# Twelve ScalarE scalings for one VectorE product: four edits to the side work of a state-space scan

## Chip, core and metric

The kernel runs on one core of a Trainium2 chip. The metric is the device time of one execution in microseconds; the kernel before has a median of 9078.85 us over 13 runs (9040.54 to 9110.47). The engines are TensorE (PE, matrix products), VectorE (DVE), ScalarE (ACT), GpSimd (POOL) and SyncE (SP, which only issues transfers). Each engine works through its own instructions in the order in which they were emitted.

## What is computed

Four images of 96 channels and 64 x 64 pixels go through four layers, each added to its input:

- **Layer 0**, a selective state-space layer. Per image a norm, a projection to 192 channels and a 3x3 convolution give u. From u come, for four directions k, the step sizes delta and the vectors B and C. Then for each channel and each of 16 states `h = exp(delta*A)*h + (delta*u)*B` runs along the 4096 pixels, and `y = sum(h*C)`. The four directions are added, normalised, gated by z and projected.
- **Layer 1**, a deformable 3x3 convolution. A convolution gives for each pixel and each of nine taps an offset and a mask. Each tap is sampled at its shifted place: four neighbouring pixels, weighted by the bilinear weights times the mask, are added. A product with the weights follows.
- **Layers 2 and 3**: a Fourier mixing (a transform over 4096 tokens, a diagonal product, the transform back), a feed-forward net with inputs rounded to 8-bit floats, a linear attention over all tokens, and a second such feed-forward net.

## The kernel before

**The scan** (`Layer0.scan`) is the backbone: 4 images x 4 directions x 4 pieces of 1024 pixels x 24 groups of 8 channels = 1536 units. In one unit, with 8 channels x 16 states on the 128 partitions, ScalarE takes `exp` of the steps (`decay`, line 933, two units ahead of the scan), TensorE spreads delta*u over the states into PSUM (`inflow`, 939, one unit ahead, two buffers), VectorE multiplies that by B (`enter`, 953) and runs the recurrence (`recur`, 961), GpSimd saves the last column (`weigh`, 968) and multiplies by C (970), and TensorE folds the states (`total`, 989). ScalarE's queue also issues the 512 KB load `da` of each unit (912).

**Side work** is put between the units by two streams (`layers23`, lines 1702 to 1750). `ends` does layer 0 up to the scan for images 0 to 3 (`Layer0.before`) and then layers 2 and 3 image by image. `middle` does, for each image, the end of layer 0 (`behind`) and layer 1 (`Layer1.image`). `ends` begins with image b's layers 2 and 3 only once layer 1 of that image is done. When the scan is over, both streams go on with each other and the unit loop stands still (`alone`); `net.own_banks` is set from there on.

**The order** of all instructions is fixed when the program is made. Each step of a stream is a Python generator step that emits instructions and yields their assumed cost per engine. A `Clock` keeps the assumed end of each engine's work. `unit` moves the due time of the next unit on by `PACE`, the least unit time. `has_room` lets a step be emitted only while the engines it uses are at most `AHEAD` (3, 3, 5, 7 us for PE, DVE, ACT, POOL) beyond now, and at most `BESIDE` = 6 us of VectorE's side work go beside one unit. `go` (1725) offers the room to the two streams in reversed order, `middle` first.

**What the change touches:**

- `steps` (752) makes delta and delta*u for 512 pixels: TensorE product `pd`, five ScalarE activations (772 to 777), two GpSimd subtractions (780, 781), the VectorE sum `rl` = delta (783), the GpSimd product with u (786, 792; for the transposed direction with a strided view), then three ScalarE casts and TensorE products that split delta*u into three 16-bit parts. Each image has 48 such chains. `lw` has one buffer.
- `sample` (1284) handles three taps of 128 pixels at a time, 96 such groups an image: three indirect gathers by GpSimd (1301) fill `g` with 12 pixels of 96 channels on each partition, one VectorE product (1310) weights them, and TensorE transposes and adds the four corners (1327). After the scan VectorE adds the corners (1314, 1315) and TensorE only transposes. ScalarE evicts (1335), TensorE multiplies by the weights (1343).
- `chunk` in `Ffn.run` (1562) does 512 tokens: GpSimd rounds the input to 8 bits (1567), TensorE, ScalarE's eviction (1573), the bias (1578 by VectorE after the scan, 1582 by ScalarE within it), GpSimd rounds again (1585), TensorE, eviction (1591), bias (1594 or 1596), sum (1598).

Of the kernel before, what the change touches and what calls it, by code (L numbers as in the profile page):

```python
# [14 lines left out]
AF = mybir.ActivationFunctionType  # L15
# [4 lines left out]
B, C, H, W = 4, 96, 64, 64  # L20
# [152 lines left out]
class Step:  # L173
# [5 lines left out]
    def __init__(self, work, wait=0.0, holds=0, new=False, takes="", frees=""):  # L179
        self.work, self.wait, self.holds, self.new = work, wait, holds, new  # L180
        self.takes, self.frees = takes.split(), frees.split()


def cost(pe=0.0, dve=0.0, act=0.0, pool=0.0, **more):
    return Step((pe, dve, act, pool), **more)


def wait(us=0.0, **more):

    return Step((0.0,) * 4, us, **more)  # L190
# [10 lines left out]

MARGIN = 0.5

PACE = 4.7


class Clock:
# [19 lines left out]
    def unit(self, scanned):  # L227

        self.due += PACE
        self.idle, self.beside = max(scanned, self.due), 0.0  # L230
# [115 lines left out]
class Net:  # L346
# [3 lines left out]
    def __init__(self, ctx, tc, ins):  # L350
        self.tc, self.nc, self.ins = tc, tc.nc, ins
        nc = self.nc
        self.const = ctx.enter_context(tc.tile_pool(name="const", bufs=1))
        self.dram = ctx.enter_context(tc.tile_pool(name="scratch", bufs=1, space=DRAM))
        self.psum = ctx.enter_context(tc.tile_pool(name="mm", bufs=3, space=PSUM))
        for name in ("vecs", "ident", "cen96", "grp3", "add4"):
            setattr(self, name, self.load(name, self.const))

        self.to_row = {}
        for n in (C, DI):  # L360
            t = self.to_row[n] = self.const.tile([128, 65], F32, name=f"to_row{n}")
            nc.vector.memset(t, 0.0)
            nc.vector.memset(t[:, 1:2], 1.0 / n)
        self.eps = self.const.tile([128, 1], F32, name="eps")
        nc.vector.memset(self.eps, 1e-5)
        self.one = self.const.tile([128, 1], F32, name="one")
        nc.vector.memset(self.one, 1.0)
        self.minus_one = self.const.tile([128, 1], F32, name="minus_one")
        nc.vector.memset(self.minus_one, -1.0)
        self.exp_and_log()  # L370

        self.sampled = set()
        self.clock, self.known, self.streams, self.stream = Clock(), {}, [], None

        self.own_banks = None
# [164 lines left out]
class Layer0:  # L540
# [211 lines left out]
    def steps(self, b, ks, j, us, dtw, sm, xdbl):  # L752

        net = self.net
        nc = net.nc
        cs = slice(j * CH, (j + 1) * CH)
        tk = f"{b}_{j}_" + "".join(str(k) for k in ks)
        both = len(ks) == 2

        def tile_of(name, bufs):  # L760
            return sm.tile([128, CH], F32, name=f"{name}{tk}", tag=name, bufs=bufs)

        yield wait(new=True, takes="ex lw")


        pd = net.mm(f"pd{tk}")
        for k in ks:
            q = k % 2
            o, m = (pd[64 * q : 64 * q + 64], slice(128, DI)) if both else (pd, slice(0, 128))
            nc.tensor.matmul(o, lhsT=dtw[:, k, m], rhs=xdbl[q, j], start=True, stop=True)  # L770
        ex = tile_of("ex", 3)
        nc.scalar.activation(ex, pd, AF.Abs)
        nc.scalar.activation(ex, ex, AF.Exp, scale=-1.0)
        lw, w1 = tile_of("lw", 1), tile_of("w1", 1)
        nc.scalar.activation(lw, ex, AF.Ln, bias=net.one)
        nc.scalar.activation(w1, ex, AF.Identity, bias=net.one)
        nc.scalar.activation(w1, w1, AF.Identity, bias=net.minus_one)  # L777
        yield cost(pe=2.2 if both else 1.1, act=3.4, holds=1, takes="rl")
        rl = tile_of("rl", 2)
        nc.gpsimd.tensor_sub(w1, w1, ex)  # L780
        nc.gpsimd.tensor_sub(lw, lw, w1)  # L781
        yield cost(pool=2.8, holds=1)
        nc.vector.scalar_tensor_tensor(rl, pd, 0.0, lw, ALU.max, ALU.add)  # L783
        yield cost(dve=0.7, frees="lw")
        if not both and ks[0] % 2:
            nc.gpsimd.tensor_mul(
                ex.rearrange("p (w h) -> p w h", h=H),
                rl.rearrange("p (w h) -> p w h", h=H),
                us[1][:, j * NR : (j + 1) * NR, :],
            )  # L790
        else:
            nc.gpsimd.tensor_mul(ex, rl, us[2 if both else 0][:, cs])  # L792
        parts = ((0, 64, ks[0], 128), (64, 128, ks[1], 128)) if both else ((0, 128, ks[0], 0),)
        for p0, p1, k, c0 in parts:
            nc.sync.dma_start(self.de_d[b][k][c0 : c0 + p1 - p0, cs], rl[p0:p1])
        yield cost(pool=1.4, takes="du", frees="rl")

        du = sm.tile([128, 3, CH], BF16, name=f"du{tk}", tag="du", bufs=2)
        nc.scalar.copy(du[:, 0, :], ex)
        yield cost(act=0.6, new=True)  # L800
        pr = net.mm(f"pr{tk}")
        nc.tensor.matmul(pr, lhsT=net.ident, rhs=ex, start=True, stop=False)  # L802
        nc.tensor.matmul(pr, lhsT=self.minus, rhs=du[:, 0, :], start=False, stop=True)
        nc.scalar.copy(du[:, 1, :], pr)
        yield cost(pe=1.5, act=0.6, holds=1, frees="ex")
        nc.tensor.matmul(
            pr, lhsT=self.minus, rhs=du[:, 1, :], start=False, stop=True, skip_group_check=True
        )
        nc.scalar.copy(du[:, 2, :], pr)
        yield cost(pe=0.4, act=0.6)  # L810
        for p0, p1, k, c0 in parts:
            dst = self.du_d[b][k][:, c0 : c0 + p1 - p0, cs]
            nc.sync.dma_start(dst.rearrange("s c t -> c s t"), du[p0:p1])
        self.ready.update((b, k, both, j) for k in ks)
        yield wait(frees="du")
# [300 lines left out]
class Layer1:  # L1116
# [23 lines left out]
    def image(self, b):  # L1140
        tc = self.net.tc
        with tc.tile_pool(name=f"l1i{b}", bufs=1, side="right") as ix:
            idx = ix.tile([128, 288], U32, name=f"idx{b}", tag="idx")
            wt = ix.tile([128, 288, 4], F32, name=f"wt{b}", tag="wt")
            yield from self.before(b, idx, wt)
            yield from self.sample(b, idx, wt)
        self.net.sampled.add(b)

# [135 lines left out]
    def sample(self, b, idx, wt):  # L1284
        net = self.net
        tc, nc = net.tc, net.nc
        with tc.tile_pool(name=f"l1g{b}", bufs=1, side="right") as gp:
# [4 lines left out]
            def taps(t, k0):  # L1292
# [4 lines left out]
                cs = slice(j * 256, (j + 1) * 256)  # L1297
                g = gp.tile([128, 3, 4 * C], F32, name=f"g{key}", tag="g", bufs=6)
                for k in range(3):
                    n = 9 * t + k0 + k  # L1300
# [4 lines left out]
                        in_offset=bass.IndirectOffsetOnAxis(ap=idx[:, n : n + 1], axis=0),  # L1305
                    )
                    yield cost(pool=1.5, wait=7.0 * (k == 2))
                g4 = g.rearrange("p k (c d) -> p (k c) d", d=C)
                w4 = wt[:, 9 * t + k0 : 9 * t + k0 + 3, :].rearrange("p k c -> p (k c)")
                nc.vector.tensor_mul(g4, g4, w4.unsqueeze(2).to_broadcast([128, 12, C]))  # L1310
                added = net.own_banks is not None
                if added:

                    nc.vector.tensor_add(g[:, :, : 2 * C], g[:, :, : 2 * C], g[:, :, 2 * C :])
                    nc.vector.tensor_add(g[:, :, :C], g[:, :, :C], g[:, :, C : 2 * C])
                first = q == 0 and k0 == 0
                yield cost(dve=2.7 if added else 1.8, new=True, takes="st" if first else "")
                if first:
                    sts[j] = gp.tile([C, 9, 256], F32, name=f"st{b}_{j}", tag="st")
                st = sts[j]  # L1320
# [210 lines left out]
class Ffn:  # L1531
# [23 lines left out]
    def run(self, b, t):  # L1555
        net, n = self.net, self.n
        tc, nc = net.tc, net.nc
        with tc.tile_pool(name=f"fb{n}_{b}", bufs=1) as big, tc.tile_pool(name=f"fs{n}_{b}", bufs=2) as pool:
            tl = big.tile([C, L], F32, name=f"fl{n}_{b}", tag="tl")
            yield from normed(net, t, tl, f"f{n}_{b}", pool)  # L1560

            def chunk(j):
                yield wait(takes="xq")
                cs = slice(j * CH, (j + 1) * CH)
                key = f"f{n}_{b}_{j}"
                xq = pool.tile([C, CH], F8, name=f"xq{key}", tag="xq")
                nc.gpsimd.tensor_copy(xq, tl[:, cs], saturate=False)  # L1567
                yield cost(pool=0.8, new=True, takes="h16")
                h16 = pool.tile([128, 3, CH], F16, name=f"h16{key}", tag="h16")
                for g in range(3):  # L1570
                    ph = net.mm(f"ph{key}_{g}")
# [10 lines left out]
                        nc.scalar.activation(h16[:, g], h16[:, g], AF.Relu, bias=self.bias[:, g : g + 1])  # L1582
                    yield cost(act=2.1, takes="h8")
                h8 = pool.tile([128, 3, CH], F8, name=f"h8{key}", tag="h8")
                nc.gpsimd.tensor_copy(h8, h16, saturate=False)
                yield cost(pool=1.5, new=True, takes="o16", frees="h16")
                po = net.mm(f"po{key}")
                for g in range(3):
                    nc.tensor.matmul(po, lhsT=self.w2[:, g, :], rhs=h8[:, g], start=(g == 0), stop=(g == 2))
                o16 = pool.tile([C, CH], F16, name=f"o16{key}", tag="o16")  # L1590
# [106 lines left out]
def layers23(net, x2, out):  # L1697
# [4 lines left out]
    with ExitStack() as ctx:  # L1702
# [19 lines left out]
        streams = net.streams = [Stream(net, ends()), Stream(net, middle())]  # L1722
        clock = net.clock

        def go():

            return any([stream.step() for stream in reversed(streams)])

        def alone():

# [5 lines left out]
        for goes in l0.scan():  # L1736
# [3 lines left out]
            if clock.own is not None:  # L1740
                clock.due = max(clock.due, clock.own + PACE)
                clock.idle = max(clock.idle, clock.due)
# [32 lines left out]
```

## Time and profile before

| what | us |
|---|---|
| median of 13 runs | 9078.85 |
| the profiled execution | 9090.48 |
| its span, first to last instruction | 9088.7 |
| first and last scan (line 961) | 365 to 7907 |
| sampling of image 0, of 1, of 2 | 2559 to 3738, 4469 to 5502, 6374 to 7340 |
| sampling of image 3, after the scan | 8077 to 8534 |
| layers 2 and 3 of image 0, of 1 (within the scan) | 4752 to 6134, 6143 to 7555 |
| layers 2 and 3 of image 2 | 7563 to 8632 |
| layers 2 and 3 of image 3 (alone) | 8632 to 9089 |
| busy, of the span: PE, DVE, ACT, POOL | 73%, 77%, 46%, 70% |

A row for a group of instructions gives line, engine, operation, the tiles written and read, and shapes; then how many, their busy time and mean duration, the idle time of the engine just before them, and what ended it. A row for a stretch of time gives start and end, length, the busy time and count for each engine, the granted TensorE clock, the busy share of the transfer engines and GB/s. Busy shares are averages over stages with different limits, so they have to be read by stage.

### The profile page before, as it was taken

How to read it: one execution, taken by the hardware profiler on the slowest of the kernel's cores; microseconds unless marked ns; L12 is line 12 of the kernel's file. 1: busy time of each engine (PE TensorE's matmuls, PEld its weight loads, DVE VectorE, ACT ScalarE, POOL GpSimd, SP SyncE). 2: the span in 40 equal slices, each digit the busy share in tenths (PEclk: the TensorE clock that was granted, in tenths of full speed). 3: DMA queues.
4: the chain of work that ended last, by engine and by line, in shares of the span. 5: the costliest groups of instructions: out<-in, count | busy, mean ns of one | idle time of the engine just before them, and what ended most of it. 6: DMA issues, size and time to landing. Idle time of an engine off the chain costs nothing.

```text
span 9088.7 us, 93197 instructions
## 1 busy us (share of the span) xinstructions
PE 6601.8 (73%) x31960; PEld 2989.1 (33%) x31960; DVE 6955.7 (77%) x4932; ACT 4186.7 (46%) x5798; POOL 6389.0 (70%) x4755
## 2 busy tenths in 40 slices
PE   6664976697766668777667787777777777874687
PEld 2111311132222234211224554223554332462373
DVE  0367878887788889788789898988999998646514
ACT  4564667565554435556543324554333434321223
POOL 0486679766788989788799896765888966538501
PEclk8775977798777779877778888888888777886797
DMA  1466788777778788787788878677888776644210
GB/s 51 130 183 166 186 197 223 197 190 187 196 205 209 206 207 219 195 207 206 200 209 207 220 205 195 171 170 193 219 212 213 189 174 171 157 131 138 72 58 12
DMA packets 775967, 1608.21 MB, mean 177 GB/s; under 512 B 247809, under 2 KB 339357, under 8 KB 773382
## 3 DMA queue, kind: packets, MB, share of 16 engines
q10 hardware_dynamic: 244224, 843.17, 37.3%
q1 hardware_dynamic: 457542, 532.51, 22.0%
q0 software_dynamic: 73728, 226.57, 9.5%
q8 instruction: 255, 4.18, 0.2%
q14 instruction: 218, 1.79, 0.1%
HBM read 1345.62 MB, written 256.29 MB: 176 GB/s over the span
## 4 chain that ended last, share of the span: by engine, by line
PE 32%; DVE 19%; DMA 16%; POOL 15%; issue 10%; ACT 6%; SPq 2%; ACTq 1%; DVEq 0%; POOLq 0%
DVE hh L961 8%; POOL hh L970 7%; DVE db L953 5%; PE pc L692 4%; PE py L989 4%; POOL g L1301 3%; PE ps L1327 3%; PE f L1421 3%; PE db L939 3%; DMA du<-du 3%; DMA da<-de 2%; PE pd L1343 2%; DVE g L1310 2%; DMA m<-in_dft 2%; DMA bc<-bcd 1%
## 5 line engine op out<-in xcount | busy, mean ns | idle before, releaser
L970 POOL TENSOR_TENSOR hh<-hh,bc 128x1024 f32<-128x1024 f32 x1536 | 3657.5, 2385 | 340.7 <-DVE hh L961 222.6
L961 DVE TENSOR_TENSOR_SCAN hh<-da,st,db 128x1024 f32<-128x1024 f32 x1152 | 2700.2, 2344 | 190.0 <-PE py L989 59.3
L953 DVE TENSOR_TENSOR db<-db,bc 128x1024 f32<-128x1024 f32 x1536 | 1864.2, 1214 | 534.0 <-PE db L939 532.0
L933 ACT ACTIVATE da<-da,w_al 128x1024 f32<-128x1024 f32 x1536 | 1740.4, 1147 | 841.8 <-DMA da<-de 403.2
L939 PE MATMUL db<-du,rep 96*128 96x512 bf16 x3072 | 1094.1, 445 | 785.8 <-DVE hh L961 711.0
L1301 POOL DMA_INDIRECT g<-table,idx x1152 | 1342.8, 1166 | 363.5 <-issue 226.1
L989 PE MATMUL py<-hh,w_fold 128*32 128x512 f32 x6144 | 1101.8, 748 | 91.2 <-POOL hh L970 59.1
L1327 PE MATMUL ps<-w_ident,g 128*96 128x128 f32 x3744 | 639.7, 333 | 509.0 <-issue 299.1
L961 DVE TENSOR_TENSOR_SCAN hh<-da,db 128x1024 f32<-128x1024 f32 x384 | 876.8, 2283 | 54.8 <-PE py L989 19.2
L939 PEld LDWEIGHTS <-rep 96*128 96x128 bf16 x3072 | 279.7, 107 | 1756.2 <-issue 1106.8
L1310 DVE TENSOR_TENSOR g<-g,wt 128x1152 f32<-128x1152 f32 x384 | 705.0, 1838 | 102.2 <-DMA g<-table,idx 101.9
L1335 ACT COPY st<-ps 96x384 f32<-96x384 f32 x384 | 182.8, 476 | 1298.2 <-PE ps L1327 1155.0
L1327 PEld LDWEIGHTS ps<-w_ident,g 128*96 128x96 f32 x3744 | 519.3, 155 | 786.6 <-issue 420.2
L968 POOL COPY st<-hh 128x1 f32<-128x1 f32 x1152 | 303.5, 263 | 518.0 <-DVE hh L961 477.7
L780 POOL TENSOR_TENSOR w<-w,ex 128x512 f32<-128x512 f32 x192 | 245.6, 1279 | 500.2 <-ACT w L777 499.6
L692 PE MATMUL pc<-pad,wc 96*128 96x512 f32 x1152 | 544.7, 612 | 48.3 <-DMA wc<-wc_d 44.1
L783 DVE SCALAR_TENSOR_TENSOR rl<-pd,lw 128x512 f32<-128x512 f32 x192 | 131.2, 683 | 422.2 <-POOL lw L781 404.4
L802 PE MATMUL pr<-ex,w_ident 128*128 128x512 f32 x384 | 284.7, 832 | 153.7 <-POOL ex L792 64.5
L1567 POOL CAST xqf<-fl 96x512 fp8e5<-96x512 f32 x64 | 44.4, 702 | 496.7 <-DVE fl L1525 459.2
L989 PEld LDWEIGHTS py<-hh,w_fold 128*32 128x32 f32 x6144 | 160.9, 121 | 616.4 <-issue 370.7
L770 PE MATMUL pd<-xd,w_dtw 103*64 103x512 f32 (+1 forms) x512 | 277.9, 830 | 69.8 <-DMA w_dtw<-in_dtw 32.1
L692 PEld LDWEIGHTS pc<-pad,wc 96*128 96x128 f32 x1152 | 217.5, 195 | 321.9 <-issue 299.4
(249 smaller groups left out, 9205.0 us busy)
## 6 DMA issues: line engine op xcount, KB each, us to landing
da<-de ACTq DMA_DIRECT2D x1536, 512.0 KB
du<-du SPq DMA_DIRECT2D x512, 192.0 KB
bc<-bcd SPq DMA_DIRECT2D x128, 512.0 KB
du<-du SPq DMA_DIRECT2D x128, 384.0 KB
y<-yb SPq DMA_DIRECT2D x384, 128.0 KB
de<-rl SPq DMA_DIRECT2D x128, 256.0 KB
m<-in_dft SPq DMA_DIRECT2D x128, 256.0 KB
ad<-y ACTq DMA_DIRECT2D x192, 128.0 KB
```

What stands on the lines that cost most here:

```text
L692: nc.tensor.matmul(pp, lhsT=wc[:, q, g * 128 : (g + 1) * 128], rhs=pad[:, r0 + dy : r0 + dy + NR, dx : dx + W], start=(q == 0), stop=(q == 8),
L802: nc.tensor.matmul(pr, lhsT=net.ident, rhs=ex, start=True, stop=False)
L933: self.net.nc.scalar.activation(u.da, u.da, AF.Exp, scale=self.al[:, a : a + 1])
L939: self.net.nc.tensor.matmul(db[:, h, :], lhsT=self.rep[:96, u.s % 4, :], rhs=u.du[u.s // 4][:, h * CH : (h + 1) * CH], start=True, stop=True,)
L953: self.net.nc.vector.tensor_mul(u.db, u.db, u.bc[:, 0, :])
L961: nc.vector.tensor_tensor_scan(u.along(u.hh), u.along(u.da), u.along(u.db), first, ALU.mult, ALU.add)
L968: self.net.nc.gpsimd.tensor_copy(u.state[:, u.n : u.n + 1], u.hh[:, last : last + 1])
L970: self.net.nc.gpsimd.tensor_mul(u.hh, u.hh, u.bc[:, 1, :])
L989: nc.tensor.matmul(py[p0 : p0 + 32], lhsT=self.fold[:, u.i, :], rhs=hc[:, h * CH : (h + 1) * CH], start=u.sums["add"] is None and u.i == 0 ...
L1301: nc.gpsimd.indirect_dma_start(out=g[:, k, :], out_offset=None, in_=self.tables[b % 2], in_offset=bass.IndirectOffsetOnAxis(ap=idx[:, n : ...
L1310: nc.vector.tensor_mul(g4, g4, w4.unsqueeze(2).to_broadcast([128, 12, C]))
L1327: nc.tensor.matmul(pt[:, k, :], lhsT=g[:, k, c * C : (c + 1) * C], rhs=net.ident, is_transpose=True, start=(c == 0), stop=(c == corners - 1),)
```

## The change

1. **Weighting**: the one product of VectorE over 12 pixels becomes 12 ScalarE activations of 96 elements with the weight as a scale per partition, in three steps of the generator. The corner sums after the scan stay with VectorE.
2. **delta times u** goes from GpSimd to VectorE.
3. **The feed-forward casts** go from GpSimd to VectorE, after the scan only.
4. **The order of the streams** is turned round, layers 2 and 3 first, from the moment the sampling of image 3 begins.
5. **PACE** goes from 4.7 to 4.5.

The assumed costs are changed to match.

```diff
-PACE = 4.7
+PACE = 4.5
...
         self.sampled = set()
+        self.sampling_last = False
...
         if not both and ks[0] % 2:
-            nc.gpsimd.tensor_mul(
+            nc.vector.tensor_mul(
...
         else:
-            nc.gpsimd.tensor_mul(ex, rl, us[2 if both else 0][:, cs])
+            nc.vector.tensor_mul(ex, rl, us[2 if both else 0][:, cs])
...
-        yield cost(pool=1.4, takes="du", frees="rl")
+        yield cost(dve=0.7, takes="du", frees="rl")
...
             yield from self.before(b, idx, wt)
+            self.net.sampling_last = b == B - 1
             yield from self.sample(b, idx, wt)
...
-                g4 = g.rearrange("p k (c d) -> p (k c) d", d=C)
-                w4 = wt[:, 9 * t + k0 : 9 * t + k0 + 3, :].rearrange("p k c -> p (k c)")
-                nc.vector.tensor_mul(g4, g4, w4.unsqueeze(2).to_broadcast([128, 12, C]))
+                for k in range(3):
+                    for c in range(4):
+                        pixel = g[:, k, c * C : (c + 1) * C]
+                        n = 9 * t + k0 + k
+                        nc.scalar.activation(pixel, pixel, AF.Identity, scale=wt[:, n, c : c + 1])
+                    if k < 2:
+                        yield cost(act=0.7)
...
-                yield cost(dve=2.7 if added else 1.8, new=True, takes="st" if first else "")
+                yield cost(dve=1.0 * added, act=0.7, new=True, takes="st" if first else "")
...
-                nc.gpsimd.tensor_copy(xq, tl[:, cs], saturate=False)
-                yield cost(pool=0.8, new=True, takes="h16")
+                if net.own_banks:
+                    nc.vector.tensor_copy(xq, tl[:, cs], saturate=False)
+                    yield cost(dve=0.4, new=True, takes="h16")
+                else:
+                    nc.gpsimd.tensor_copy(xq, tl[:, cs], saturate=False)
+                    yield cost(pool=0.8, new=True, takes="h16")
...
-                nc.gpsimd.tensor_copy(h8, h16, saturate=False)
-                yield cost(pool=1.5, new=True, takes="o16", frees="h16")
+                if net.own_banks:
+                    nc.vector.tensor_copy(h8, h16, saturate=False)
+                    yield cost(dve=1.0, new=True, takes="o16", frees="h16")
+                else:
+                    nc.gpsimd.tensor_copy(h8, h16, saturate=False)
+                    yield cost(pool=1.5, new=True, takes="o16", frees="h16")
...
-            return any([stream.step() for stream in reversed(streams)])
+            return any([stream.step() for stream in (streams if net.sampling_last else streams[::-1])])
```

## The prediction

> **What bounds the kernel now.** I read the list of costliest groups first, then the busy time of the engines by stage, then the timeline inside a stage, then who waited for whom.
>
> Four groups, from the page (columns: busy us, mean ns of one | idle just before, and what ended it):
>
> ```profile
> L970 POOL TENSOR_TENSOR hh<-hh,bc 128x1024 f32<-128x1024 f32 x1536 | 3657.5, 2385 | 340.7 <-DVE hh L961 222.6
> L961 DVE TENSOR_TENSOR_SCAN hh<-da,st,db 128x1024 f32<-128x1024 f32 x1152 | 2700.2, 2344 | 190.0 <-PE py L989 59.3
> L1301 POOL DMA_INDIRECT g<-table,idx x1152 | 1342.8, 1166 | 363.5 <-issue 226.1
> L1310 DVE TENSOR_TENSOR g<-g,wt 128x1152 f32<-128x1152 f32 x384 | 705.0, 1838 | 102.2 <-DMA g<-table,idx 101.9
> ```
>
> Each of the 1536 units of the recurrence needs 2.33 + 1.21 = 3.55 us of VectorE (scan L961, multiply L953) and about 2.39 + 0.2 us of GpSimd (L970, L968). The scans run from 365 to 7907 us: 7542 / 1536 = 4.91 us a unit, well over either. What fills the rest differs by stage. The three long lines below are the sampling of images 0, 1 and 2 inside the scan; then the sampling of image 3 after it, then layers 2 and 3 of image 3 alone:
>
> ```profile
> core 0: us, PE busy (x) PEld busy (x) DVE busy (x) ACT busy (x) POOL busy (x), PEclk, DMA share, GB/s
> 2559.00:3738.00 1179.00, 848.36 (x3614) 382.59 (x3616) 1051.87 (x642) 536.26 (x673) 1061.54 (x772) 0.82 0.81 210
> 4469.00:5502.00 1033.00, 776.00 (x4880) 445.73 (x4881) 938.91 (x594) 376.80 (x496) 937.13 (x686) 0.83 0.82 209
> 6374.00:7340.00 966.00, 740.10 (x4775) 442.48 (x4768) 891.76 (x556) 357.22 (x489) 866.85 (x637) 0.84 0.81 206
> ...
> 8077.00:8534.00 457.00, 245.84 (x1160) 165.12 (x1158) 301.08 (x374) 91.74 (x184) 358.94 (x305) 0.69 0.47 137
> ...
> 8632.00:9089.00 457.00, 378.00 (x3028) 266.67 (x3028) 128.81 (x185) 137.27 (x270) 39.15 (x33) 0.86 0.12 35
> ```
>
> In the three sampling stretches (3178 us, 637 scans: 4.99 us a unit) VectorE is busy 2883 us (91%) and GpSimd 2866 us (90%); GpSimd also loses 0.2 us at each gather ("issue", 226.1 us over 1152), 170 us for 864 gathers, so it is really full at 3035 us (95%). ScalarE is at 40%. Two engines are full together; the third is not.
>
> Why L1310 has a mean of 1838 ns when its shortest is 1327 shows in the timeline of a full stretch (start, us, engine):
>
> ```profile
> 5445.70 2.36 POOL L970 TENSOR_TENSOR hh<-hh,bc 128x1024 f32<-128x1024 f32 x1
> 5445.97 3.30 DVE L1310 TENSOR_TENSOR g<-g,wt 128x1152 f32<-128x1152 f32 x1
> 5448.00 1.32 POOL L968 COPY st<-hh 128x1 f32<-128x1 f32 x1
> ```
>
> The weighting started just after GpSimd's product and took 3.30 us; then GpSimd's one-column copy, 0.19 us elsewhere, took 1.32 until the weighting was over. Each holds the other up.
>
> **The change part by part.**
>
> *Weighting, in the scan.* Off VectorE: 288 of L1310, 201.5 + 182.4 + 191.3 = 575 us. VectorE falls to 2307 of 3178 us (73%). Off GpSimd: L968 took 170 us in these stretches for 464 copies against 0.187 us each before sampling began (52.1 / 279), so 83 us. On ScalarE: 12 activations of 128x96 with a pointer for a scale, per group. No such row exists. Below: the 128x108 eviction from PSUM of L1221 without a pointer, started every 0.146 us back to back; above: the one 128x96 activation on SBUF (L555), 0.283 us. I take 0.22, midway since it has the source of the one and the back-to-back run of the other: 2.6 us a group, 760 us for 288 (500 to 980), which brings ScalarE in these stretches from 1270 to 2030 us (64%; 56 to 71%). So the work itself stays off the end-setting path.
>
> [...]
>
> The change also moves a wait. VectorE waited 101.9 us (60 times) for gathers to land; now ScalarE does. Queued behind that wait on ScalarE are the decays (L933), the evictions L1335, and the issue of the da loads; the scan waits for the decays. The cover is that a decay is issued two units ahead (about 9.5 us); the longest of these waits was 7.1 us, and 83.9 of the 101.9 us lie after the scan, so 18 within it. I cost it at 0; gone, it is the slower rival below.
>
> *What is late next.* GpSimd. With the same mix its stretch cannot go under 3035 - 83 = 2952 us, a gain of 226 at most. At a realistic 96.5% it is 3059 us, a gain of 119. But the least unit time also thins the mix: in the clock a unit of 4.5 us has room for (4.5 - 2.55) / 1.5 = 1.3 gathers, against 864 / 637 = 1.36 seen, so 666 units instead of 637. If those run at 4.65 us, the middle of what stretches with little VectorE side work show (4.1 to 5.0), it is 3097 us against 3178 + 29 x 4.7 = 3314, a gain of 217. I take the middle, **-170** (0 to -226).
>
> *delta times u.* Off GpSimd: L786 and L792, 99.1 + 168.8 = 268 us. On VectorE: 192 products with both inputs in SBUF, 128x512. The nearest rows are L423 (693 ns when GpSimd is idle) and L1598 (1203 mean, 1870 beside a GpSimd operation); L1310 lost (2.00 - 1.35) = 0.65 us on average in the scan. I take 0.69 + 0.65 = 1.34 us, 257 us (133 to 359). In the first stretch (365 to 888 us, 5.39 us a unit) a chain takes 485 / 48 = 10.1 us, in which GpSimd has two units (5.2), two subtractions (2.6) and this product (1.4): 9.2 us, the fullest engine. Without the product the next limit is the single lw buffer (five activations, two subtractions, one add: some 8 us). About 40 chains by 0.9: **-35** (0 to -56). The other 144 trade 200 us of a GpSimd that idles 0.3 to 0.5 us a unit there against 193 us of a VectorE that idles 0.5 to 1.1: 0 (-60 to +95).
>
> *The least unit time.* 1536 x 0.2 = 307 us less of planned room, so 4% less side work beside each unit. Stretches with more side work have longer units, by 0.2 to 0.5 us per us of side work of VectorE and GpSimd (a fit over blocks of 32 units); with 1.5 us of it outside sampling and 800 units that is **-20** (0 to -30). The work not done is layers 2 and 3 of image 2: an image of these takes 1380 to 1412 us within the scan and 457 alone, so 307 us of room is 22% of one, 100 us alone, after the scan.
>
> *After the scan.* Sampling of image 3 ends at 8534, image 2 leaves at 8632, and only then do 457 us of image 3 follow. While sampling goes first, TensorE is busy 246 of 457 us and VectorE idles 83.9 us for landing gathers; nothing runs for most of those 98 us but image 2. With layers 2 and 3 first, the 290 us (alone) of image 2 that I expect to be left at 8077, the 100 above included, go into that stage. Sampling needs at least 288 x (1.177 + 0.2) = 397 us of GpSimd, and ScalarE then has 253 us of weighting on top of 92 plus about 110 of image 2. I give the stage 480 us instead of 457 + 98: **-75**, of which 20 are taken back for ScalarE's queue, -55 (0 to -110).
>
> *Casts by VectorE after the scan*, 32 chunks. The rows from 8534 on:
>
> ```profile
> L1578 DVE TENSOR_SCALAR h16f<-h16f,bias 128x512 f16<-128x512 f16 x72 | 36.1, 557 | 1.4 <-ACT h16f L1573 1.2
> L1598 DVE TENSOR_TENSOR t<-t,o16f 96x512 f32<-96x512 f32 x24 | 34.2, 1427 | 0.8
> ```
>
> VectorE hardly waits here: 3 x 0.557 + 0.627 (L1594) + 1.427 = 3.73 us a chunk, and it is slowed by GpSimd's casts (0.34, 0.34 and 0.69 undisturbed, so 2.05). The casts add between 0.34 + 1.0 (rate of L1578) and 0.69 + 2.07 (rate of L423); I take 0.43 (L422, 512 f32) + 1.0. 3.48 against 3.73: **-5** (-10 to +35).
>
> Sum: -170 - 35 - 20 - 55 - 5 = -285. The profiled span is 9088.7 in an execution of 9090.5, which is 11.6 over the median of 9078.9. 9090.5 - 285 - 11.6 = 8794, so **8795**.
>
> **The rivals.**
>
> 1. *GpSimd and the transfers become the bound.* For: GpSimd is at 95% in sampling, and the transfer engines at 0.81 to 0.82. Against: units of 4.1 to 4.6 us occur in stretches with as much TensorE work. Then only the 83 us of L968 and half of the tail's 60 come: 9079 - 113 = 8966.
> 2. *Slower: ScalarE's queue.* A group of 12 activations that meets a late gather holds decays, evictions and da loads. The place is the 288 groups in the scan. A group that is hit costs the scan its wait, on VectorE 101.9 / 60 = 1.7 us, and some 1 us of its own work: 2.7 us. It decides from 285 / 2.7 = 106 hit groups on; with half of them, 144, it is 9079 - 285 + 389 = 9185. For: ScalarE already waits 403 us for da. Against: the lead of two units.
> 3. *More than forecast.* Gathers thin out, units go to 4.5 us in and beside sampling, and the tail gives its whole 110: 8650.
> 4. *Nothing moves*: what VectorE is freed of returns as waits on TensorE (L953 waited 532.0 us for L939): 9080.
>
> **How the numbers follow.** Forecast 0.52 (8700 to 8900), rival 1 0.20, rival 3 0.10, rival 4 0.03, slower 0.15. About 0.2% (18 us) is what a measurement of this kernel can tell from no change. Faster 0.82, same 0.03, slower 0.15. The range 8640 to 9060 holds the forecast, rivals 1 and 3; it leaves out the slower case and no change.
>
> **What would show it.** In the changed profile: VectorE under 80% in the sampling stretches with GpSimd over 90%; the mean of L968 near 0.19; units near 4.7 us there; the new products near 1.3 us; activations of 96 elements near 0.2 us; image 2 leaving before sampling ends; 457 us of image 3 kept. I am wrong if the decays' waits on gathers grow to hundreds of us, if scans wait for da, or if image 2 leaves long after sampling.

## The result, and the profile after

The changed kernel takes 9109.06 us (median of 11 runs, 9088.39 to 9124.91) against 9073.8 for the kernel before (median of 48 runs): ratio 1.0039, 95% interval 1.0027 to 1.0051. It is slower by 0.4%, where 3% faster was forecast. The profiled execution of it took 9083.5 us (span 9081.7), 26 below its median, and that of before 9090.5, 17 above its own; so a difference of 40 us cannot be read from this pair, and only stages that moved by more are.

First the group of activations that replaced L1310, then stages of the changed kernel: the sampling of images 0, 1, 2; from the last scan to the last sampling; the last sampling; image 3 alone. Columns as before.

```profile
L1314 ACT ACTIVATE g<-g,wt 128x96 f32<-128x96 f32 x4608 | 1285.0, 366 | 160.7 <-DMA du<-du 34.2
```

```profile
2601.00:3882.00 1281.00, 963.36 (x3966) 398.88 (x3967) 1055.42 (x664) 932.05 (x1950) 1069.99 (x839) 0.82 0.84 220
4565.00:5708.00 1143.00, 901.52 (x5913) 498.93 (x5906) 948.34 (x608) 736.40 (x1725) 944.06 (x753) 0.83 0.87 221
6390.00:7529.00 1139.00, 885.82 (x5916) 500.18 (x5913) 932.32 (x589) 736.20 (x1748) 935.01 (x748) 0.85 0.85 213
7769.00:7977.00 208.00, 165.56 (x1252) 103.34 (x1246) 51.26 (x86) 72.21 (x132) 34.85 (x31) 0.85 0.39 96
7977.00:8534.00 557.00, 394.10 (x2488) 288.67 (x2487) 188.02 (x319) 418.33 (x1397) 288.62 (x289) 0.69 0.42 124
8630.00:9082.00 452.00, 364.42 (x3028) 256.44 (x3028) 127.25 (x217) 137.06 (x270) 3.83 (x1) 0.90 0.12 36
```

The scan did gain: the last scan ends at 7769 us instead of 7907. In sampling VectorE fell from 91% to 82%, GpSimd from 90% to 83% (1070 + 944 + 935 of 3563 us), and a unit from 5.01 to 4.57 us (counted from the first gather to the last eviction: 780 units in 3563 us against 628 in 3144). But the sampling stretches now hold 780 units, and the 756 units outside them take 5.07 us instead of 4.84, which fits that the same convolutions and end parts of layer 0 stand beside fewer units. And after the scan all is lost again: the last sampling takes 557 us instead of 457, with ScalarE at 75%, and layers 2 and 3 of image 2 start at 7804 instead of 7563, so that image 3 is alone from 8630 as before (8633).

Neither VectorE nor GpSimd is full in sampling now. The waits in the sampling of image 2 (us in total, times, longest), in the kernel before and then in the changed one:

```profile
POOL st L968 <- DVE hh L961: 7.3, 3, 3.5
DVE db L953 <- PE db L939: 45.4, 29, 4.1
```

```profile
POOL st L969 <- DVE hh L962: 73.6, 27, 13.4
DVE db L954 <- PE db L940: 132.3, 53, 12.0
```

GpSimd now waits for scans, and VectorE for the inflow from TensorE: in the three sampling stretches together 354 us instead of 148.

### The profile page after: what moved, and what is told of

The parts are those of the page before. It is cut to its first block, busy times and chain, and to the rows that moved or that the text cites. A ratio compares the mean times of both kernels' runs of the same rounds, so it can differ in the third digit from the quotient of the medians.

```text
span 9081.7 us, 98417 instructions
## 1 busy us (share of the span) xinstructions
PE 6677.1 (74%) x31960; PEld 2937.7 (32%) x31960; DVE 6591.0 (73%) x4806; ACT 5374.3 (59%) x10405; POOL 5806.1 (64%) x4498
## 5 line engine op out<-in xcount | busy, mean ns | idle before, releaser
L1303 POOL DMA_INDIRECT g<-table,idx x1152 | 1155.8, 1003 | 496.2 <-issue 173.2
L1314 ACT ACTIVATE g<-g,wt 128x96 f32<-128x96 f32 x4608 | 1285.0, 366 | 160.7 <-DMA du<-du 34.2
L990 PE MATMUL py<-hh,w_fold 128*32 128x512 f32 x6144 | 1069.7, 760 | 38.0 <-POOL hh L971 19.8
L1333 PE MATMUL ps<-w_ident,g 128*96 128x128 f32 x3744 | 685.3, 325 | 345.0 <-ACT g L1314 161.6
L1333 PEld LDWEIGHTS ps<-w_ident,g 128*96 128x96 f32 x3744 | 489.7, 143 | 697.2 <-ACT g L1314 295.6
L969 POOL COPY st<-hh 128x1 f32<-128x1 f32 x1152 | 251.3, 218 | 535.9 <-DVE hh L962 485.5
L1320 DVE TENSOR_TENSOR g<-g 128x576 f32<-128x576 f32 x96 | 72.8, 758 | 356.8 <-ACT g L1314 333.3
L1349 PE MATMUL pd<-st,wdc 96*128 96x256 f32 x1152 | 305.4, 412 | 10.5 <-ACT st L1341 8.9
```

The source lines that it names most:

```text
L990: nc.tensor.matmul(py[p0 : p0 + 32], lhsT=self.fold[:, u.i, :], rhs=hc[:, h * CH : (h + 1) * CH], start=u.sums["add"] is None and u.i == 0 ...
L1303: nc.gpsimd.indirect_dma_start(out=g[:, k, :], out_offset=None, in_=self.tables[b % 2], in_offset=bass.IndirectOffsetOnAxis(ap=idx[:, n : ...
L1314: nc.scalar.activation(pixel, pixel, AF.Identity, scale=wt[:, n, c : c + 1])
L1333: nc.tensor.matmul(pt[:, k, :], lhsT=g[:, k, c * C : (c + 1) * C], rhs=net.ident, is_transpose=True, start=(c == 0), stop=(c == corners - 1),)
L1349: nc.tensor.matmul(po, lhsT=wdc[:, k, :], rhs=st[:, k, :], start=(k == 0), stop=(k == 8))
```

## The experiments

Letters for the parts: **W** weighting by ScalarE, **M** delta times u, **C** casts, **O** order, **P** PACE 4.5. All parts and no others, W+M+C+O+P, is the changed kernel. Stages are read from the profiled execution of each, in us; the last sampling is counted from the first gather to the last eviction (454 us before, where the stretch shown above takes 457); "alone from" is the moment at which image 3's layers 2 and 3 begin. The kernels were not all measured on one chip, and the medians of the kernel before beside them lie between 9057 and 9105 us. So kernels are compared by their ratios, and a difference of ratios is given in us as a share of 9074. A profiled execution can lie off its median, most of all that of e6 (9273 us, 70 above) and that of e17 (8906, 47 below).

| kernel | scan ends | last sampling | image 0's layers 2, 3 begin | image 2's begin | alone from | median | ratio (95%) |
|---|---|---|---|---|---|---|---|
| before | 7907 | 454 | 4778 | 7563 | 8633 | | 1 |
| changed | 7769 | 557 | 4741 | 7804 | 8630 | 9109 | 1.0039 (1.0027 to 1.0051) |
| e1: W | 7805 | 601 | 4612 | 7372 | 8718 | 9179 | 1.0132 (1.0095 to 1.0170) |
| e2: P | 7797 | 428 | 5300 | 8435 | 8893 | 9312 | 1.0266 (1.0233 to 1.0299) |
| e3: M | 8053 | 448 | 4669 | 7636 | 8779 | 9251 | 1.0210 (1.0174 to 1.0245) |
| e4: W+M+C+O | 7896 | 567 | 4509 | 7463 | 8647 | 9113 | 1.0053 (1.0029 to 1.0077) |
| e5: W in the scan | 7827 | 465 | 4634 | 7391 | 8551 | 8996 | 0.9912 (0.9882 to 0.9943) |
| e6: W+C+O+P | 7674 | 616 | 5199 | 7941 | 8808 | 9203 | 1.0130 (1.0096 to 1.0163) |
| e7: W in the scan, M+C+O+P | 7816 | 508 | 4759 | 7854 | 8583 | 9023 | 0.9936 (0.9912 to 0.9960) |
| e8: W in the scan, C+O | 7832 | 449 | 4637 | 7389 | 8464 | 8925 | 0.9824 (0.9791 to 0.9856) |
| e9: P, GpSimd's room kept | 7894 | 447 | 5123 | 7982 | 8811 | 9254 | 1.0168 (1.0145 to 1.0191) |
| e10: W in the scan, O | 7844 | 486 | 4638 | 7404 | 8517 | 8978 | 0.9854 (0.9821 to 0.9888) |
| e11: W, priced | 7753 | 470 | 4736 | 7371 | 8581 | 9029 | 0.9920 (0.9897 to 0.9943) |
| e12: M, priced | 8106 | 464 | 4418 | 7671 | 8846 | 9297 | 1.0224 (1.0188 to 1.0259) |
| e13: P, VectorE's assumed time cut | 7840 | 472 | 5373 | 8571 | 9009 | 9457 | 1.0374 (1.0327 to 1.0421) |
| e14: M, one step | 8100 | 424 | 4661 | 7613 | 8786 | 9245 | 1.0163 (1.0132 to 1.0193) |
| e15: as e14, input from PSUM | 7984 | 426 | 4549 | 7498 | 8669 | 9144 | 1.0054 (1.0033 to 1.0076) |
| e16: all, W priced | 7800 | 569 | 4812 | 7841 | 8758 | 9198 | 1.0100 (1.0068 to 1.0131) |
| e17: W priced, C+O | 7715 | 514 | 4723 | 7337 | 8440 | 8952 | 0.9850 (0.9803 to 0.9898) |
| e18: W in the scan, priced, C+O | 7743 | 463 | 4736 | 7355 | 8418 | 8869 | 0.9740 (0.9691 to 0.9788) |

### Single parts (e1 to e4)

The edits are the hunks of the diff above, each part with its assumed costs.

> Part 1 alone on the kernel before: ScalarE weights the gathered pixels, in the scan and after it, PACE 4.7. Theory A (the scan gains from the weighting, the stage after it pays: work put off by the smaller least unit time, and ScalarE's 3.2 us a group in the last sampling): the scan ends near 7800 us, the last sampling takes some 520 us instead of 457, in all about 9000. Theory B (the weighting is worth what was forecast, and the product delta*u on VectorE eats it): about 8900, with the scan ending near 7700.

> Part 5 alone on the kernel before: PACE 4.5. Theory A: units no shorter than their work allows, so the scan ends at most 60 us sooner, layers 2 and 3 of image 2 begin some 150 us later, and the whole takes 9074 + 60 = about 9135. Theory B: no more than 15 us either way from 9074.

> Part 2 alone on the kernel before: the product delta times u by VectorE. Theory A: what GpSimd is spared and VectorE pays are alike, within 20 us of 9074. Theory B: the products take 1.65 us beside GpSimd and hold up the scans queued behind them, 192 x 0.7 = 130 us, about 9200.

> The whole change but with PACE 4.7. Theory A: the work put off comes back into the scan, layers 2 and 3 of image 2 begin before the scan ends, about 9020. Theory B: PACE did little, so as the whole change, about 9110.

W and P fit neither of their theories. M did what its Theory B told, and more: products of 1.52 us on average, and a scan that ends 146 us later. Each of the three alone is slower than before, W by 1.3%, P by 2.7% and M by 2.1%, and the whole change loses 0.4%: the parts do not add. e4 came as its Theory B: PACE, some 240 us worse alone, is worth nothing in company (from e4 to the changed kernel the scan ends 127 us sooner, and what follows is 117 us longer). Three separate losses had to be found.

### The weighting after the scan (e5, e7, e11)

```diff
 e5, on the kernel before: the old product where net.own_banks is set, else the 12 activations
 e7: the same on the changed kernel
 e11, e16, e17, e18: the cost in the clock of four activations, here and in the last of the three steps
-                        yield cost(act=0.7)
+                        yield cost(act=1.07)
```

> The kernel before, with ScalarE weighting the pixels only while the scan runs; after it VectorE's one product as before. PACE 4.7, no other part. Theory A (ScalarE's 12 activations a group are what stretched the last sampling from 457 to some 600 us; in the scan they pay): the scan ends at about 7800 us, the last sampling is back at 430 to 460 us, image 2 leaves at about 8480, in all about 8930. Theory B (what the scan gained is only side work put off, and comes back after it whoever weights): sampling stays over 520 us or image 2 leaves after 8600, 9050 or more.

> The whole change, but after the scan VectorE weights the pixels. Theory A: the scan is unchanged (ends near 7770), the last sampling falls from 557 to about 450 us, then image 2 is what ends last of the two, some 60 us sooner as ScalarE is free: about 9040. Theory B (the order of the streams stretches the last sampling, not the weighting): sampling stays near 550 us, 9100.

> Part 1 alone (ScalarE weights everywhere) with the cost of four activations in the clock at 1.07 us as measured (4 x 0.267) instead of 0.7. Theory A (the work itself fills ScalarE in the last sampling): the last sampling stays over 550 us, 9150 to 9200. Theory B (the wrong price made the clock queue too much on ScalarE ahead of the rest): the last sampling falls under 500 us and the whole under 9050.

e1 and e5 differ only after the scan: ratios 1.0132 and 0.9912. So the weighting after the scan cost 2.2%, some 200 us, and in the scan it pays 0.9%. In e7 the same undoing brings the changed kernel from 1.0039 to 0.9936 (93 us); its sampling came down by half of what was expected (508 us). My explanation, that ScalarE was full, was wrong: in e1's last sampling it is busy 370 of 601 us. The timeline of e1 shows one full round there (start, us, engine; in brackets the idle time before and what ended it), and below it are two waits of the whole stage:

```profile
8309.45 0.47 ACT L1339 COPY st<-ps 96x384 f32<-96x384 f32 x1 [2.27 <-PE ps L1331]
8309.82 3.29 ACT L1312 ACTIVATE g<-g,wt 128x96 f32<-128x96 f32 x12
8310.16 0.94 POOL L1301 DMA_INDIRECT g<-table,idx  x1 [2.48 <-ACT st L1339]
...
8313.15 0.76 DVE L1318 TENSOR_TENSOR g<-g 128x576 f32<-128x576 f32 x1 [4.68 <-ACT g L1312]
8313.94 0.46 DVE L1319 TENSOR_TENSOR g<-g 128x288 f32<-128x288 f32 x1
8314.65 0.85 PE L1331 MATMUL ps<-w_ident,g 128*96 128x128 f32 x3 [5.24 <-DVE g L1319]
8315.53 0.47 ACT L1339 COPY st<-ps 96x384 f32<-96x384 f32 x1 [2.42 <-PE ps L1331]
8315.91 3.29 ACT L1312 ACTIVATE g<-g,wt 128x96 f32<-128x96 f32 x12
```

```profile
DVE g L1318 <- ACT g L1312: 437.9, 95, 7.5
ACT st L1339 <- PE ps L1331: 226.6, 92, 4.8
```

It is a closed round of 6.1 us: 12 activations (3.29), two adds by VectorE, three transposes, the eviction by ScalarE, and only then the next 12. While the adds and transposes run, ScalarE stands for 2.4 us before an eviction that was emitted ahead of the next weighting, and the gathers wait 2.5 us until it is over. 96 rounds of 6.1 us are 586 of the 601 us. No engine is full (after ScalarE come GpSimd with 291 us, TensorE with 194 and VectorE with 146); one queue is in the wrong order. With the right price (e11) the clock emits the weighting of two groups before the evictions:

```profile
8256.93 0.48 ACT L1339 COPY st<-ps 96x384 f32<-96x384 f32 x1 [2.06 <-PE ps L1331]
8256.94 0.95 POOL L1301 DMA_INDIRECT g<-table,idx  x1 [0.31 <-PE ps L1331]
8257.31 6.51 ACT L1312 ACTIVATE g<-g,wt 128x96 f32<-128x96 f32 x24
...
8263.71 0.47 ACT L1339 COPY st<-ps 96x384 f32<-96x384 f32 x1
```

24 activations stand in one run, the first eviction follows with no wait, and the round over two groups takes some 9.0 us (from the start of these 24 to the next run at 8266.33). The last sampling falls to 470 us and the scan ends 52 us sooner as well. The expectation on record, that the work itself filled ScalarE, fell with that.

### What the order, the casts and a right price are worth (e8, e10, e16 to e18)

> What should remain of the change by Theory A: ScalarE weights in the scan, VectorE after it, the order of the streams and the casts as changed; delta times u with GpSimd and PACE 4.7 as before. Theory A: about 8900, the fastest so far. Theory B (the order and the casts are worth nothing or less): as the run with the weighting in the scan alone, or slower.

> ScalarE weights in the scan, VectorE after it, and the order of the streams as changed; casts as before, PACE 4.7. Theory A (the order lets image 2 run beside the last sampling; the casts are worth some 25 us more, from GpSimd's queue and from VectorE being held up by its casts): 8950, between 8996 without both and 8925 with both. Theory B (the gain of 71 us is the casts', as layers 2 and 3 no longer queue behind the gathers): 8990.

> The whole change with four activations at their measured 1.07 us in the clock instead of 0.7. Theory A (the wrong price is what undid the weighting): the last sampling falls from 557 to under 490 us and the whole from 9109 to about 9000. Theory B (with layers 2 and 3 first the price matters little): 9080 to 9120.

> ScalarE weights everywhere, priced at 1.07 us for four; order and casts as changed; delta times u with GpSimd, PACE 4.7. Theory A (price mended, parts 2 and 5 dropped): 9029 less the 71 us of order and casts, about 8950. Theory B (after the scan ScalarE is still too full beside layers 2 and 3): 9030 or more.

> As the fastest so far (ScalarE weights in the scan only, order, casts, PACE 4.7, 8925), with the price at 1.07 us for four. Theory A (a right price helps within the scan too: the scan of the run with the price mended ended at 7753 instead of 7805): about 8870. Theory B (it only matters after the scan): 8925 within 25 us.

e8, e10, e17 and e18 lie near their Theory A. From e5 to e8 the order and the casts bring the ratio from 0.9912 to 0.9824. e10, with the order alone, lies between (0.9854); its interval overlaps that of e8, so the casts' share is not told from nothing. What the casts do is seen on the rows from 8534 on in the changed kernel:

```profile
L1588 DVE TENSOR_SCALAR h16f<-h16f,bias 128x512 f16<-128x512 f16 x72 | 27.6, 438 | 0.0
L1596 DVE CAST h8f<-h16f 128x1536 fp8e5<-128x1536 f16 x24 | 23.0, 957 | 1.0
...
L1612 DVE TENSOR_TENSOR t<-t,o16f 96x512 f32<-96x512 f32 x24 | 16.5, 688 | 0.8
...
L1574 DVE CAST xqf<-fl 96x512 fp8e5<-96x512 f32 x24 | 9.6, 419 | 6.1 <-PE phf L1582 6.1
L1608 DVE TENSOR_SCALAR o16f<-o16f,bias 96x512 f16<-96x512 f16 x24 | 8.3, 345 | 11.8 <-ACT o16f L1605 11.8
```

The casts add 0.42 + 0.96 = 1.38 us a chunk to VectorE. The sum L1612 has gone from 1427 to 688 ns, the three biases L1588 from 557 to 438 and the bias L1608 from 627 to 345, together 1.38 us as well: VectorE's own busy time is as before. That it was GpSimd's casts that held these up is the likely reason, which no run tested by itself.

For the time of image 3 alone it is not enough to be even. Here are e5, without the casts, and e18, with them, in that stage:

```profile
8551.40:8994.00 442.60, 363.11 (x3028) 256.44 (x3028) 128.84 (x185) 137.10 (x270) 39.07 (x33) 0.90 0.12 37
```

```profile
8418.00:8883.00 465.00, 378.12 (x3028) 265.34 (x3028) 127.17 (x217) 137.34 (x270) 3.83 (x1) 0.86 0.12 35
```

The stage goes with the granted clock, so kernels with the same clock have to be compared: at 0.90 it takes 443 us in e5 and 452 in the changed kernel, at 0.86 457 before and 465 in e18. With the casts it is 8 to 9 us longer; no run changed them alone.

e18 is the fastest kernel found, 8869 us, with a right price and without M and P. After its scan come 205 us up to the first gather, a sampling of 463 us and a tail of 465 us, image 3 alone. e16 missed: with M and P in place the right price does not help (sampling 569 us, ratio 1.0100). Why it is even slower than the changed kernel is not settled.

The price is not all of it. e17 and e18 differ only in who weights after the scan, both with the right price: 0.9850 and 0.9740. So with layers 2 and 3 first the weighting by ScalarE after the scan costs 1.1% at the right price and 1.0% at the wrong one (the changed kernel against e7). Without the order and the casts it costs nothing at the right price (e11 0.9920, e5 0.9912). The likely reason is that ScalarE's queue then holds the evictions of image 2 between the weightings; no run tested that by itself. In the last sampling of the changed kernel VectorE waits for the activations less often than in e1, but longer:

```profile
DVE g L1320 <- ACT g L1314: 333.3, 83, 23.0
```

### delta times u (e3, e12, e14, e15, e6)

```diff
 e12
-        yield cost(dve=0.7, takes="du", frees="rl")
+        yield cost(dve=1.5, takes="du", frees="rl")
 e14: the product by VectorE directly behind the sum rl, one step
-        yield cost(dve=0.7, frees="lw")
...
+        yield cost(dve=1.4, frees="lw")
...
 e15: the same, with another input (here and for the transposed direction)
-            nc.vector.tensor_mul(ex, rl, us[2 if both else 0][:, cs])
+            nc.vector.tensor_mul(ex, pd, us[2 if both else 0][:, cs])
```

> Part 2 alone with the product's cost in the clock at 1.5 us of VectorE as measured instead of 0.7. Theory A (the product itself and its lock with GpSimd cost the scan, whatever the clock assumes): the scan ends over 8000, about 9230. Theory B (the clock put a product before scans that it thought short): the scan ends under 7950, about 9120.

> Part 2 alone with the product emitted in one step with the sum before it, as a base for the next run. Both theories: as part 2 alone, 9220 to 9300.

> As the run before, but the product takes pd from PSUM in place of delta from SBUF: it computes u times the unrectified step, so the softplus is left out of delta times u. Same length, one SBUF input only. Theory A (the cost is the hold-up between VectorE and GpSimd that two SBUF inputs bring): the product takes 0.68 us instead of 1.5, and the whole is about 9110. Theory B (the product lengthens the chain of a step and VectorE's queue, lock or not): 9200 or more.

> The whole change without part 2 (delta times u stays with GpSimd), PACE 4.5. Theory A (part 2 costs the scan what it cost alone, some 146 us): the scan ends near 7640, about 8980. Theory B (with VectorE freed of the weighting, part 2 costs nothing, and the tail is what is lost): within 30 us of the whole change, 9080 to 9140.

Alone, M ends the scan 146 us later, and the right price does not mend it (e12, Theory A). The products in e14, then in e15, in each the transposed direction first and then one of the two groups of the others:

```profile
L785 DVE TENSOR_TENSOR ex<-rl,xa 128x512 f32<-128x512 f32 x64 | 115.8, 1810 | 5.2 <-ACT ex L773 0.5 <-DVE rl L783 0.5
L791 DVE TENSOR_TENSOR ex<-rl,xa 128x512 f32<-128x512 f32 x64 | 96.2, 1503 | 5.4 <-ACT ex L773 0.5
```

```profile
L785 DVE TENSOR_TENSOR ex<-pd,xa 128x512 f32<-128x512 f32 x64 | 66.2, 1034 | 0.0
L791 DVE TENSOR_TENSOR ex<-pd,xa 128x512 f32<-128x512 f32 x64 | 43.5, 680 | 0.0
```

With one input from PSUM the mean over all 192 falls from 1598 to 798 ns, the scan ends 116 us sooner, and the ratio goes from 1.0163 to 1.0054, nearer to Theory A. So two thirds of what M costs in e14 come with the second SBUF input. The 0.5% left go with a product of 0.8 us in VectorE's queue; what part of M they come from was not separated. e6 missed: at PACE 4.5 the kernel without M is 0.9% slower (83 us), not faster. In its profiled execution, 70 us over its median as it is, the scan does end 95 us sooner without M, but layers 2 and 3 begin at 5199 instead of 4741. The softplus chains that come before them in `ends` fall behind: the last product of delta and u starts at 5184 instead of 4728 us. That it is the product that finds no room with GpSimd is the likely reason. As far as these runs show, M is paid for in the scan and earns its price only where P has taken that room.

### The least unit time (e2, e9, e13)

```diff
 e9 (and PACE 4.5)
-        u.weighed = self.net.clock.add(POOL, 2.55, self.scanned[0])
+        u.weighed = self.net.clock.add(POOL, 2.35, self.scanned[0])
 e13 (and PACE 4.5)
-        self.scanned = (self.scanned[1], clock.add(DVE, 2.33, max(u.decayed, free)))
+        self.scanned = (self.scanned[1], clock.add(DVE, 2.13, max(u.decayed, free)))
```

> PACE 4.5 on the kernel before, with GpSimd's product of a unit (L970) assumed to take 2.35 us in the clock instead of 2.55 (measured: 2.39), so that the room left to GpSimd's side work beside a unit is 2.15 us again as with 4.7. Theory A (the smaller least unit time hurt because it took the room from GpSimd's side work, the gathers and the softplus chains, so that layers 2 and 3 of image 0 began at 5300 instead of 4778 us): they begin before 4900, and the whole falls from 9312 to 9050 to 9120. Theory B (any side work has 4% less room, whichever engine): still over 9250.

> PACE 4.5 on the kernel before, with the recurrence (L961) assumed to take 2.13 us of VectorE in the clock instead of 2.33, so that VectorE's room beside a unit is 1.15 us again; GpSimd's assumed cost as before. Theory A (the loss is VectorE's room, 1.15 to 0.95 us, 17% less, while GpSimd's falls 9%): layers 2 and 3 of image 0 begin before 4950 and the whole is 9080 to 9150. Theory B (no one engine's room; each holds it): 9230 or more.

P alone ends the scan 110 us sooner, but puts the stream of `ends` off by much more than its 4%: image 0's layers 2 and 3 begin 522 us later, image 2's at 8435 instead of 7563, when everything else is over. It falls behind while images 0 and 1 are sampled: the products of delta and u of image 2 end at 3453 instead of 3211 us, those of image 3 at 5268 instead of 4763. In the end two images run alone, one after the other, 458 us from 8435 to 8893 and as much again. e9 shows that GpSimd's room is part of it: image 0's layers begin 177 us sooner, a third of what was lost, and the ratio falls from 1.0266 to 1.0168; by the time that is still Theory B. e13 went the wrong way (1.0374). By the code of `Clock`, a smaller assumed VectorE time also lowers "now", from which the room of all engines is counted. Which other room holds that stream is open.

## Why the prediction was wrong

The forecast of 8795 us is a ratio of 0.969; 1.0039 is 3.5% more, some 320 us. Three steps of undoing account for most of it: VectorE weights again after the scan (e7, 93 us), M and P go (e8, 102 us), and the activations get their right price (e18, 76 us).

- **After the scan.** This is the step that failed most, and it turned the sign: 480 us given to a stage that took 653 (7977 to 8630). The work left of image 2 was as forecast: begun at 7804, it had 457 - 173 = 284 us to go if alone, against 290. ScalarE's time was added up (253 + 92 + 110) and found to fit, but in one queue the weighting has to take turns with evictions that wait for VectorE and TensorE, and a sum of busy times says nothing of that. Shown are the price of it (e7; e17 against e18) and the closed round in W alone (e1, e11); how the turns fall beside image 2 is not shown.
- **delta times u.** "-35" and "0" failed. The product takes 1.52 us instead of 1.34, and in the first stretch, where 35 us were to be gained, the second direction starts at 902 instead of 888: taking the product off GpSimd shortened nothing there. Alone the part ends the scan 146 us later. Idle VectorE time outside sampling was counted as free; it is not, since a shorter product brings the scan back by 116 us (e15).
- **The least unit time.** "-20", with 100 us of image 2 absorbed after the scan, failed. It works by when the side streams get their turn, and that is not 4% of anything: the start of image 2's layers 2 and 3 moves by 872 us alone, by 341 us in company (e4 to the changed kernel, 7463 to 7804).
- **Cost of the weighting.** 0.22 us per activation was forecast, 0.265 to 0.267 from start to start was measured (busy 1285 us for 4608; 366 ns from start to end): 966 us in the scan instead of 760, within the bounds. The lower bound was no back-to-back run: after an eviction L1221 the next instruction, of another line, often starts 0.146 us later (15 of 32 times), but two of these evictions are never less than 3.2 us apart. That such work stays off the path that sets the end as long as ScalarE is not full was wrong, since 0.267 against the 0.175 in the clock's prices decides how ScalarE's queue is laid out (e1 to e11: 2.1%, some 190 us).
- **The wait for gathers.** Right: no decay was held by it that mattered; waits of L933 for da went from 403 to 367 us. The activations themselves stood idle for 161 us in all, no more than 34 of them for any one cause. The slower rival, built on this, was not the cause.
- **What is late next.** The unit in sampling came near, 4.57 us against 4.65, but not for the reason given. GpSimd was to be the full engine at 96.5% and is at 88%, the 0.2 us lost at each gather counted as in the forecast (83% without). VectorE's waits for TensorE's inflow have grown instead, as in the rival in which nothing moves. The unit lies near the least unit time of the plan: 4.57 us at 4.5, and 4.65 at 4.7 with all else alike (e4). What bounds it is not shown, so the size was luck in part. The number of units in sampling (666 forecast, 780 measured) and the price outside it (5.07 instead of 4.84) were not foreseen; the scan became 142 us shorter instead of 225.
- **Casts.** The sizes were right: 0.42 + 0.96 us, forecast as 0.43 + 1.0. The gain of 5 us was not: that image 3 alone takes 452 us instead of 457 goes with a granted clock of 0.90 instead of 0.86, and at the same clock the casts make it some 8 us longer.

## What to carry to other kernels

Where the order of instructions is planned by assumed costs, moving work to another engine moves the plan too: measure the new instruction first and put its real start-to-start time into the plan, since a price a third too low turned a gain of 0.8% into a loss of 1.3% (e11, e1). Price a move stage by stage: the same weighting gains where the giving engine is full and loses where it has to take turns in one queue with what drains the same chain, beside other work even at the right price (e17, e18). And try the parts of a change alone and in company, for here each of three lost more alone than all together, and the best version holds two parts and half of a third, at the right price.

## What the runs showed of the hardware

- A VectorE product of 128x512 with two SBUF inputs took 1.5 us on average beside a working GpSimd and 0.68 us with one input from PSUM; with the u view of the transposed direction it took 1.81 and 1.03 us, the latter 0.35 more for the same number of elements (e14, e15).
- ScalarE started 96-element activations every 265 to 267 ns, although each took 363 ns from start to end (median of 4608 in the changed kernel).
- Without VectorE's weighting in the scan GpSimd's one-column copies fell from 263 to 191 ns on average (e5), and the mean of a gather's issue from 1166 to 1028 ns (e5; 1003 in the changed kernel).
- The same work, image 3 alone without the casts, took 443 us at a granted TensorE clock of 0.90 (e5) and 457 at 0.86 (the kernel before).
